# A Mamba block with a feed-forward layer: sines, rotation, carried states and the final sum rewritten on ScalarE and GpSimd

## The chip, the cores and the metric

The kernel runs on one core of a Trainium2 chip. The core's engines run side by side, each with its own queue of instructions in program order: TensorE (PE, with its weight loads as PEld), VectorE (DVE), ScalarE (ACT), GpSimd (POOL) and SyncE (SP), which here only issues DMAs. They wait for each other by semaphores. The metric is the device time of one execution in microseconds; the time before is the median of three runs.

## The reference

The input is x, 2 sequences of 4096 tokens of width 256. First a layer norm and a Mamba-like layer, then a feed-forward layer, each added to x through a further layer norm. What matters here:

```python
Bn = _rmsnorm(B_raw + B_bias, B_norm_w)
Cn = _rmsnorm(C_raw + C_bias, C_norm_w)
dt = softplus(dt_in * W_dt[:, 0] + b_dt)
freqs = softplus(rope_freqs)
angles = cumsum(mean(dt, axis=-1, keepdims=True), axis=1) * freqs
cos_a, sin_a = cos(angles), sin(angles)
# _rope, for B and for C, over pairs (ve, vo) of neighbouring states:
re = ve * cos_a - vo * sin_a
ro = ve * sin_a + vo * cos_a
# scan over the tokens, 512 channels x 16 states:
h = dA * h + u
y = sum(h * C, axis=-1)
...
x = x + layernorm(mamba(layernorm(x)))
x = x + layernorm(ffn(layernorm(x)))
```

So for each token there are 8 angles, and B and C have 16 states each, which are turned in 8 pairs. The last line is the final sum.

## The kernel before

**Blocks and units.** The tokens are cut into 16 blocks (NB) of T = 512, eight to a sequence. A block's scan is 64 units: 4 groups of 128 channels (j) x 4 rounds of states (q) x 4 (c). A unit is 128 partitions x 512 tokens: 32 channels x 4 states on the partitions, the tokens along the row.

**What a unit needs.** `decay` (L1021 on) lets ACT write the decay da = exp(dt * A) into PSUM; four such tiles exist, and it is made for the unit after the next one at most. `inputs` (L1030) lets POOL multiply b with v for two units into a tile g, of which there are three. `unit_scan` (L1043, L1046) runs the recurrence on DVE. For some units of a round (SPLIT) the scan stays in da and DVE multiplies by c (`product_v`, L1060, with the last column copied to hl by L1061); for the others POOL multiplies by c (`product_g`, L1056), and ACT copies the last column (`last`, L1050, tile hl). `sum_states` (L1072) adds up the states on PE, and thereby frees g. A sequence's later blocks start from the states that the block before left (hl): `carry` makes the tile ini, and `initial` (L1016) adds hl to it, one channel group at a time.

**Order.** It is written out by hand. Each unit has three places in a timetable; the tables AT, AT_FIRST and LAG say at which place of the running block each step of the *next* block (norm, projections, softplus, angles, sines, rotation, loads) and of the block *before* (output projection, feed-forward layer, final sum) is issued. Each engine takes its instructions in that order. SP issues all loads and stores of the loop in order too. `silu_z` stands at place 151, `sines` at 153, `rotate_a` at 155, `rotate_b` and `bc_turn` at 157, `bc_store` at 160; between 151 and 153 no decay is issued. `initial` is issued for channel group 0 at unit 0, and for group j + 1 at the first unit of the last round of group j.

**Sines and rotation.** DVE brings the angles into [-pi, pi] (`angles`, tile ang, 128 x 32: 4 x 128 tokens x 8 angles). ACT takes Sin of it (sn) and of half of it (cs); POOL makes the cosine, 1 - 2 sin^2 of the half angle, by L822 and L823, four products of 64 elements (L832 to L835), and the difference and sum into rot (L841, L842). L844 multiplies the turned B and C (bdotc). PE transposes rot (L850), ACT copies it (L854), and SP writes it to DRAM, from where the b and c of all units of the next block are loaded.

**Tables.** ACT evaluates functions from a table set that has to be loaded. `special` (L220 on) loads the set of Exp and Ln by hand (L223); for all other functions the load is put in automatically and stands under the line of the activation (L227).

**Final sum.** `finish` (L1208) lets POOL add o2 to the tile xpost, 512 elements a row at a time, and SP writes it out. xpost is loaded by `x_load`. The tiles of b and c begin two floats ahead of the data (L983 on, `t[:, 2:]`); xpost doesn't.

Of the kernel before, what the change touches and what calls it, by code (L numbers as in the profile page):

```python
# [8 lines left out]
F32 = mybir.dt.float32  # L9
AF = mybir.ActivationFunctionType  # L10
ALU = mybir.AluOpType
# [3 lines left out]
P = 128  # L15
G = 32
T = 512
NC4 = T // P
DM = 256
DI = 512  # L20
NJ = DI // P
NS = 16
NG = P // G
NQ = NS // NG
# [7 lines left out]
PI2_HI = 6.28125  # L32
PI2_MID = 0.0019350051879882812
PI2_LO = 3.0199159819567517e-07

GBUFS = 3
DA_PSUM = 4
# [136 lines left out]
def mamba_ffn_kernel(  # L174
# [25 lines left out]
    nc = tc.nc  # L200
    B, L, _ = x.shape
# [4 lines left out]
    small = ctx.enter_context(tc.tile_pool(name="small", bufs=2))  # L206
    p1 = ctx.enter_context(tc.tile_pool(name="p1", bufs=1))
# [10 lines left out]
    table = [None]  # L218

    def special(dst, src, f, **kw):  # L220
        if f in (AF.Exp, AF.Ln):
            if table[0] != "ln_exp":
                nc.scalar.preload_act_table_set("natural_log_exp_and_others")  # L223
            table[0] = "ln_exp"
        else:
            table[0] = f
        nc.scalar.activation(dst, src, f, **kw)  # L227

    def mm_tile(shape, name):
# [2 lines left out]
    def tokens(ap, k):  # L232
        b, t0 = k // NBLK, (k % NBLK) * T
        return ap[b, t0 : t0 + T, :].rearrange("(c p) d -> p c d", p=P)

    def x_load(k, tag):
        if tag == "h1":

            xt = p1.tile([P, NH, T], F32, tag="h1", name=f"xpre_{k}")
            xt = xt[:, 0:2, :].rearrange("p a (b d) -> p (a b) d", d=DM)  # L240
        else:
            xt = p1.tile([P, NC4, DM], F32, tag=tag, name=f"{tag}_{k}")
        nc.sync.dma_start(xt, tokens(x, k))
        return xt

# [14 lines left out]
    ones = const.tile([P, P], F32, name="ones")  # L260
# [364 lines left out]
    def new_block(k):  # L625
        s = Block()
        s.k, s.first = k, k % NBLK == 0
        s.bc_d = tc.dram_tile([2 * NS, T], F32, name=f"bc_d_{k}")
        s.dt_d = tc.dram_tile([DI, T], F32, name=f"dt_d_{k}")
        s.v_d = tc.dram_tile([DI, T], F32, name=f"v_d_{k}")  # L630
        s.pz, s.dt, s.dtT, s.dx, s.vs, s.ph, s.bcq, s.ch, s.g = {}, {}, {}, {}, {}, {}, {}, {}, {}
        s.p2, s.ff, s.pq, s.ps, s.ys = {}, {}, {}, {}, {}
        return s
# [157 lines left out]
    H = NS // 2  # L791

    def angles(s):
# [14 lines left out]
        nc.vector.tensor_scalar_sub(tn, turns, ROUND)  # L808
        for part in (PI2_HI, PI2_MID, PI2_LO):
            nc.vector.scalar_tensor_tensor(ang, tn, -part, ang, ALU.mult, ALU.add)  # L810
        nc.vector.tensor_scalar(s.ang, ang, -3.1415925, 3.1415925, ALU.max, ALU.min)

    def sines(s):
        k = s.k
        s.sn = small.tile([P, NC4, H], F32, tag="sn", name=f"sn_{k}")
        s.cs = small.tile([P, NC4, H], F32, tag="cs", name=f"cs_{k}")
        special(s.sn, s.ang, AF.Sin)
        special(s.cs, s.ang, AF.Sin, scale=0.5)

    def rotate_a(s):  # L820
        k, sn, cs = s.k, s.sn, s.cs
        nc.gpsimd.tensor_mul(cs, cs, cs)  # L822
        nc.gpsimd.tensor_scalar(cs, cs, -2.0, 1.0, ALU.mult, ALU.add)  # L823
        pairs = s.bc.rearrange("p c s (h two) -> p c s h two", two=2)
        ve, vo = pairs[:, :, :, :, 0], pairs[:, :, :, :, 1]
        snb = sn[:, :, None, :].to_broadcast([P, NC4, 2, H])
        csb = cs[:, :, None, :].to_broadcast([P, NC4, 2, H])
        s.tt = [
            small.tile([P, NC4, 2, H], F32, tag=f"t{i}", name=f"t{i}_{k}", bufs=1)
            for i in range(4)  # L830
        ]
        nc.gpsimd.tensor_mul(s.tt[0], ve, csb)  # L832
        nc.gpsimd.tensor_mul(s.tt[1], vo, snb)
        nc.gpsimd.tensor_mul(s.tt[2], ve, snb)
        nc.gpsimd.tensor_mul(s.tt[3], vo, csb)  # L835

    def rotate_b(s):
        k, tt = s.k, s.tt
        s.rot = small.tile([P, NC4, 2 * NS], F32, tag="rot", name=f"rot_{k}")
        rp = s.rot.rearrange("p c (s h two) -> p c s h two", s=2, two=2)  # L840
        nc.gpsimd.tensor_sub(rp[:, :, :, :, 0], tt[0], tt[1])  # L841
        nc.gpsimd.tensor_add(rp[:, :, :, :, 1], tt[2], tt[3])  # L842
        s.bdotc = small.tile([P, NC4, NS], F32, tag="bdotc", name=f"bdotc_{k}", bufs=1)
        nc.gpsimd.tensor_mul(s.bdotc, s.rot[:, :, 0:NS], s.rot[:, :, NS : 2 * NS])  # L844

# [145 lines left out]
    def load_ch(s, j, what):  # L991

        src = s.dt_d if what == "dtr" else s.v_d
        t = scan.tile([P, NG, T], F32, tag=what, name=f"{what}_{s.k}_{j}")
        for n in range(NG):
            nc.sync.dma_start(
                t[n * G : (n + 1) * G],
                src[j * P : (j + 1) * P, :].rearrange("(c i) t -> i c t", i=G),
            )
        s.ch[j, what] = t  # L1000
# [12 lines left out]

    def initial(s, prev, j):

        nc.gpsimd.tensor_add(s.ini[:, j], s.ini[:, j], prev.hl[:, j])  # L1016

    das = {}

# [366 lines left out]
    def plan_behind(s):  # L1386

        plan = Plan(AT, 3 * (s.k + 1) * NU)
        add = plan.add

        def begin():
            s.x = x_load(s.k, "xpost")
            s.sums = small.tile([P, NC4], F32, tag="hsum", name=f"hsum_{s.k}")

        def norm():

            s.nh = Norm(s.x, 1.0 + LN_EPS, LN_EPS * LN_EPS, f"h{s.k}")
            s.nh.stats((0, 1))

        add("x_load", begin)  # L1400
        for h in range(2):
            add("out_project", out_project, s, h, i=h)
            add("out_square", out_square, s, h, i=h)
            add("out_power", out_power, s, h, i=h)
            add("residual", residual, s, h, i=h)
        add("h_stats", norm, i=0)
        add("h_stats", lambda: s.nh.stats((2, 3)), i=1)
        add("h_power", lambda: s.nh.power())
        add("h_offset", lambda: s.nh.offset())
        for h in range(2):  # L1410
            add("h_apply", lambda h=h: s.nh.apply((2 * h, 2 * h + 1)), i=h)
        for h in range(2):
            add("h_turn", lambda h=h: s.nh.turn(h), i=h)
            add("h_evict", lambda h=h: s.nh.evict(h), i=h)
        for f in range(NH):
            add("ffn_1", ffn_1, s, f, i=f)
            add("ffn_keep", ffn_keep, s, f, i=f)
        for h in range(2):
            add("gelu", gelu, s, h, i=h)
        for c in range(NC4):  # L1420
            add("ffn_2", ffn_2, s, c, i=c)
            add("ffn_sums", ffn_sums, s, c, i=c)
            add("ffn_out", ffn_out, s, c, i=c)
            add("ffn_square", ffn_square, s, c, i=c)
            if c % 2 == 1:
                h = c // 2
                add("ffn_power", ffn_power, s, h, i=h)
                add("ffn_scale", ffn_scale, s, h, i=h)
                add("finish", finish, s, h, i=h)
        return plan.done()  # L1430
# [26 lines left out]
    for what, lags in LAG.items():  # L1457
        for u in range(len(units)):
            j, q, c = units[u][1:]
            n = SPLIT[q]  # L1460
# [48 lines left out]
    def at_place(place):  # L1509
        behind(place)  # L1510
        for plan in plans:
            plan.run(place)

    for base in range(NB * NU + BEHIND):
        k, m = base // NU, base % NU
        j, q, c = m // (NQ * NG), m // NG % NQ, m % NG
        cur, prev = blocks.get(k), blocks.get(k - 1)
        if m == 0:
            if k + 1 < NB:
                blocks[k + 1] = new_block(k + 1)  # L1520
                blocks[k + 1].xpre = xnext
                plans.append(plan_ahead(blocks[k + 1], cur))
            if 0 < k < NB:
                plans.append(plan_behind(prev))
        if cur is not None:
            if q == 0 and c == 0 and j == 0 and not cur.first:
                initial(cur, prev, 0)
            if m == (LOAD_FIRST if k + j == 0 else j * NQ * NG) and j < NJ - 1:
                load_ch(cur, j + 1, "dtr")
                load_ch(cur, j + 1, "vr")  # L1530
            if q == NQ - 1 and c == 0 and j < NJ - 1 and not cur.first:
                initial(cur, prev, j + 1)
        at_place(3 * base)
        if cur is not None:
            ahead(base + AHEAD_DA, "da", 1, decay)
            ahead(base + AHEAD_U, "u", 2, inputs)
        at_place(3 * base + 1)
        if cur is not None:
            unit_scan(cur, j, q, c)
        at_place(3 * base + 2)  # L1540
        if base == NB * NU - 10:
            tail_load(cur)
        if m == X_AT and k + 2 < NB:
            xnext = x_load(k + 2, "h1")
# [49 lines left out]
```

## Time and profile before

| | |
|---|---|
| median of three runs (2022.16 to 2025.43) | 2024.63 us |
| profiled execution | 2027.52 us |
| its span, first to last instruction | 2025.8 us |
| mean granted TensorE clock | 0.931 |
| one block in the steady part | about 117 us |
| busy in 117 us of it (873 to 990 us): PE, DVE, ACT, POOL | 103.89, 110.14, 100.10, 110.10 us |
| table loads: L223, L227, L564 | 80, 80, 1, of 1283 ns each |
| sn, cs: Sin of 128 x 32 elements | 213 ns each, 16 times |
| L822, L823 (128 x 32) | 239, 217 ns, 16 times |
| L832 to L835, L841, L842, L844 (128 x 64) | 319 to 325 ns, 16 times each |
| L1016 (128 x 16) | 223 ns, 56 times |

The page's fifth part has such groups: line, engine, operation, tile written and read with the elements of a row, count, busy time, mean of one, and the idle time of the engine just before, with what ended it. The fourth part follows the work that ended last back to what released it. A timeline row gives start and duration in us, and in brackets how long the engine stood still before it. Busy shares are averages over the whole span, with a prologue of some 55 us in which little runs on POOL and DVE, and a tail of some 60 us.

### The profile page before, as it was taken

Reading aid. Unit: us, or ns where it says so; the run is one execution under the profiler, and the core shown is the slowest. Engines: PE = TensorE matmul, PEld = TensorE weight load, DVE = VectorE, ACT = ScalarE, POOL = GpSimd, SP = SyncE. Lnnn points to the kernel's source line nnn. Section 1 sums busy time; section 2 is a strip of 40 time slices with the busy share of each in tenths; the row PEclk is TensorE's granted clock in tenths of the full one; section 3 lists DMA queues with packets and bytes.
Section 4 is the critical chain, followed back from the end, with each engine's and each line's share of the span. In section 5 each row is a group of like instructions: output and inputs, shape, how many; then the busy total and the mean of one; then the engine's idle time right before and its main releaser. Section 6 shows DMA issues by size and latency. Waiting matters only on the chain.

```text
span 2025.8 us, 28291 instructions
## 1 busy us (share of the span) xinstructions
PE 1739.3 (86%) x8670; PEld 1039.7 (51%) x8670; DVE 1769.0 (87%) x2834; ACT 1624.4 (80%) x3358; POOL 1786.3 (88%) x1171
## 2 busy tenths in 40 slices
PE   6776988898989989898898988898898989887688
PEld 3433555464645536464554646465464646545256
DVE  1778999999999989899998989999899999989861
ACT  4766887979888797888879788887979888796654
POOL 3688899999989999999999999999999989999970
PEclk7867999999999999999999999999999999999798
DMA  4734446364444635444464545346454534545300
GB/s 98 181 93 105 105 120 153 92 159 105 116 104 124 158 93 150 104 119 105 123 157 103 139 104 132 110 110 152 104 137 105 140 102 115 147 104 135 75 21 11
DMA packets 155722, 233.39 MB, mean 115 GB/s; under 512 B 30161, under 2 KB 55825, under 8 KB 155569
## 3 DMA queue, kind: packets, MB, share of 16 engines
q1 hardware_dynamic: 153440, 230.80, 45.6%
q0 software_dynamic: 544, 0.71, 0.3%
q8 instruction: 68, 1.11, 0.2%
q14 instruction: 86, 0.70, 0.1%
q10 hardware_dynamic: 1584, 0.07, 0.1%
HBM read 188.51 MB, written 42.99 MB: 114 GB/s over the span
## 4 chain that ended last, share of the span: by engine, by line
ACT 38%; DVE 18%; PE 13%; POOL 11%; DMA 10%; issue 7%; SPq 2%; DVEq 0%; ACTq 0%; POOLq 0%
ACT da L227 12%; DVE g L1046 6%; POOL g L1030 6%; DMA vr<-v_d 5%; ACT L227 5%; DVE da L1043 4%; ACT L223 3%; ACT h L1134 3%; DMA xpre<-in_L_attn_x_dram 2%; POOL g L1056 2%; ACT dt L227 2%; PE y L1072 2%; PE pdtT L779 2%; DVE g L1060 2%; PE pz L639 2%
## 5 line engine op out<-in xcount | busy, mean ns | idle before, releaser
L1030 POOL TENSOR_TENSOR g<-b,vr 128x1024 f32<-128x1024 f32 x512 | 1019.0, 2002 | 43.3 <-PE y L1072 15.6
L1046 DVE TENSOR_TENSOR_SCAN g<-da,ini,g 128x512 f32<-128x512 f32 x560 | 709.9, 1272 | 48.0 <-ACT da L227 37.2
L227 ACT ACTIVATE da<-dtr,aneg 128x512 f32<-128x512 f32 x1024 | 683.6, 683 | 83.7 <-DVE g L1046 46.2
L1056 POOL TENSOR_TENSOR g<-c,g 128x1024 f32<-128x1024 f32 (+1 forms) x256 | 627.3, 2453 | 63.4 <-ACT hl L1050 56.7
L1043 DVE TENSOR_TENSOR_SCAN da<-da,ini,g 128x512 f32<-128x512 f32 x336 | 421.9, 1274 | 39.4 <-POOL g L1030 23.1
L1072 PE MATMUL y<-g,fold 128*32 128x512 f32 x2048 | 339.5, 665 | 24.9 <-POOL g L1056 14.7
L1146 PE MATMUL pf<-w2q,h 128*128 128x257 f32 x1024 | 312.9, 387 | 18.2 <-DVE o L1184 14.9
L1123 PE MATMUL ph<-oT_h,w1q 128*128 128x512 f32 x480 | 242.1, 639 | 24.1 <-ACT oT_h L595 13.1
L639 PE MATMUL pz<-oT_a,wi 128*128 128x512 f32 x512 | 250.1, 626 | 10.2 <-ACT zs L657 4.9
L1060 DVE TENSOR_TENSOR g<-da,c 128x512 f32<-128x512 f32 x384 | 257.2, 670 | 0.0
L1155 PEld LDWEIGHTS pf<-h 128*128 128x128 f32 x1024 | 194.6, 190 | 27.2
L1155 PE MATMUL pf<-h 128*128 128x128 f32 x1024 | 196.7, 274 | 0.0
L1146 PEld LDWEIGHTS pf<-w2q,h 128*128 128x128 f32 x1024 | 155.1, 191 | 53.0 <-DVE o L1184 33.5
L639 PEld LDWEIGHTS pz<-oT_a,wi 128*128 128x128 f32 x512 | 92.9, 195 | 156.8 <-issue 88.1
L1123 PEld LDWEIGHTS ph<-oT_h,w1q 128*128 128x128 f32 x480 | 89.1, 201 | 156.2 <-issue 75.8
L1072 PEld LDWEIGHTS y<-g,fold 128*32 128x32 f32 x2048 | 49.1, 112 | 139.8 <-POOL g L1056 48.6
L1092 PE MATMUL po<-wo,zs 128*128 128x256 f32 x480 | 111.6, 386 | 0.0
L911 PE MATMUL ps<-mix,dtT 128*128 128x129 f32 (+1 forms) x512 | 79.3, 301 | 34.2 <-DVE remdot L879 27.0
L911 PE MATMUL pw<-ddot,dtT 128*128 128x128 f32 (+1 forms) x512 | 84.7, 315 | 27.5 <-DVE dx L974 23.2
L1092 PEld LDWEIGHTS po<-wo,zs 128*128 128x128 f32 x480 | 88.7, 190 | 36.8 <-issue 26.0
L1046 DVE TENSOR_TENSOR_SCAN g<-da,g 128x512 f32<-128x512 f32 x80 | 96.6, 1211 | 12.6 <-ACT da L227 12.2
L779 PE MATMUL pdtT<-ident,dt 128*128 128x128 f32 x256 | 54.6, 357 | 57.7 <-ACT dtT L787 32.6
(234 smaller groups left out, 2458.2 us busy)
## 6 DMA issues: line engine op xcount, KB each, us to landing
dtr<-dt_d SPq DMA_DIRECT2D x256, 256.0 KB, 5.0
vr<-v_d SPq DMA_DIRECT2D x256, 256.0 KB, 7.0
dt_d<-dt SPq DMA_DIRECT2D x64, 256.0 KB, 2.1
v_d<-v SPq DMA_DIRECT2D x64, 256.0 KB, 4.6
b<-bc_d SPq DMA_DIRECT2D x256, 64.0 KB, 2.1
c<-bc_d SPq DMA_DIRECT2D x256, 64.0 KB, 2.6
xpre<-in_L_attn_x_dram SPq DMA_DIRECT2D x16, 512.0 KB, 4.5
xpost<-in_L_attn_x_dram SPq DMA_DIRECT2D x15, 512.0 KB, 3.9
```

The costliest lines, as they stand in the source:

```text
L227: nc.scalar.activation(dst, src, f, **kw)
L639: nc.tensor.matmul(s.pz[e], lhsT=wi[:, kk, e * P : (e + 1) * P], rhs=s.na.oT[:, kk, :], start=(kk == 0), stop=(kk == 1),)
L1030: nc.gpsimd.tensor_mul(s.g[j, q][:, hs, :], s.bcq[0, q][:, None, :].to_broadcast([P, 2, T]), s.ch[j, "vr"][:, hs, :],)
L1043: nc.vector.tensor_tensor_scan(da, da, g, ini, ALU.mult, ALU.add)
L1046: nc.vector.tensor_tensor_scan(g, da, g, ini, ALU.mult, ALU.add)
L1056: nc.gpsimd.tensor_mul(g, s.bcq[1, q][:, None, :].to_broadcast([P, NG - n, T]), g)
L1060: nc.vector.tensor_mul(s.g[j, q][:, c, :], da, s.bcq[1, q])
L1072: nc.tensor.matmul(s.ys[j][c * G : (c + 1) * G, :], lhsT=fold, rhs=g[:, c, :], start=False, stop=(q == NQ - 1), skip_group_check=True,)
L1092: nc.tensor.matmul(s.p2[h][:, i, :], lhsT=s.zs[j][:, c * P : (c + 1) * P], rhs=wo[:, j, :], start=(j == 0), stop=(j == NJ - 1),)
L1123: nc.tensor.matmul(s.ph[f], lhsT=w1q[:, kk, f * P : (f + 1) * P], rhs=s.nh.oT[:, kk, :], start=(kk == 0), stop=(kk == 1),)
L1146: nc.tensor.matmul(po[:, 0 : DM + 1], lhsT=gT, rhs=w2q[:, f, :], start=(f == 0), stop=(f == NH - 1), skip_group_check=True,)
L1155: nc.tensor.matmul(po[:, DM + 1 :], lhsT=gT, rhs=gT, start=False, stop=False, skip_group_check=True,)
```

## The change

1. `special` loads by hand also "silu_and_others" for Silu and Sin.
2. `sines` makes on ACT what the rotation needs: sn holds -sin and sin side by side, cs the cosine twice, both 16 wide. That is three Sin, a Square and an Identity with scale -2 and a bias of 1. `rotate_a` and `rotate_b` are then four POOL operations: the whole of B and C times the cosine (128 elements), the swapped halves times -sin and sin (two of 64), and one sum (128).
3. `initial` adds group 0 as before and groups 1 to 3 in one operation, at the last round of group 0.
4. xpost begins two floats into its tile, so that it and o2 are 8 bytes apart in the row.

No entry of the timetable is changed.

```diff
+TABLES = {
+    AF.Exp: "natural_log_exp_and_others",
+    AF.Ln: "natural_log_exp_and_others",
+    AF.Silu: "silu_and_others",
+    AF.Sin: "silu_and_others",
+}
...
     def special(dst, src, f, **kw):
-        if f in (AF.Exp, AF.Ln):
-            if table[0] != "ln_exp":
-                nc.scalar.preload_act_table_set("natural_log_exp_and_others")
-            table[0] = "ln_exp"
-        else:
-            table[0] = f
+        name = TABLES.get(f)
+        if name is not None and table[0] != name:
+            nc.scalar.preload_act_table_set(name)
+        table[0] = name or f
         nc.scalar.activation(dst, src, f, **kw)
...
-            xt = p1.tile([P, NC4, DM], F32, tag=tag, name=f"{tag}_{k}")
+            xt = p1.tile([P, NC4 * DM + 2], F32, tag=tag, name=f"{tag}_{k}")
+            xt = xt[:, 2:].rearrange("p (c d) -> p c d", d=DM)
...
     def sines(s):
         k = s.k
-        s.sn = small.tile([P, NC4, H], F32, tag="sn", name=f"sn_{k}")
-        s.cs = small.tile([P, NC4, H], F32, tag="cs", name=f"cs_{k}")
-        special(s.sn, s.ang, AF.Sin)
-        special(s.cs, s.ang, AF.Sin, scale=0.5)
+        s.sn = small.tile([P, NC4, H, 2], F32, tag="sn", name=f"sn_{k}", bufs=1)
+        s.cs = small.tile([P, NC4, H, 2], F32, tag="cs", name=f"cs_{k}", bufs=1)
+        special(s.sn[:, :, :, 0], s.ang, AF.Sin, scale=-1.0)
+        special(s.sn[:, :, :, 1], s.ang, AF.Sin)
+        half = small.tile([P, NC4, H], F32, tag="half", name=f"half_{k}", bufs=1)
+        special(half, s.ang, AF.Sin, scale=0.5)
+        nc.scalar.activation(half, half, AF.Square)
+        nc.scalar.activation(
+            s.cs, half[:, :, :, None].to_broadcast([P, NC4, H, 2]), AF.Identity, scale=-2.0, bias=ones[:, 0:1]
+        )
...
     def rotate_a(s):
-        nc.gpsimd.tensor_mul(cs, cs, cs)
-        nc.gpsimd.tensor_scalar(cs, cs, -2.0, 1.0, ALU.mult, ALU.add)
...
-        nc.gpsimd.tensor_mul(s.tt[0], ve, csb)
-        nc.gpsimd.tensor_mul(s.tt[1], vo, snb)
-        nc.gpsimd.tensor_mul(s.tt[2], ve, snb)
-        nc.gpsimd.tensor_mul(s.tt[3], vo, csb)
+        nc.gpsimd.tensor_mul(s.tt[0], s.bc, cs[:, :, None, :].to_broadcast([P, NC4, 2, NS]))
+        for i in range(2):
+            nc.gpsimd.tensor_mul(
+                turned_pairs[:, :, :, :, i],
+                pairs[:, :, :, :, 1 - i],
+                sn[:, :, None, :, i].to_broadcast([P, NC4, 2, H]),
+            )
...
     def rotate_b(s):
-        nc.gpsimd.tensor_sub(rp[:, :, :, :, 0], tt[0], tt[1])
-        nc.gpsimd.tensor_add(rp[:, :, :, :, 1], tt[2], tt[3])
+        nc.gpsimd.tensor_add(
+            s.rot.rearrange("p c (s n) -> p c s n", s=2), tt[0], tt[1]
+        )
...
     def initial(s, prev, j):
-        nc.gpsimd.tensor_add(s.ini[:, j], s.ini[:, j], prev.hl[:, j])
+        js = slice(j, j + 1) if j == 0 else slice(j, NJ)
+        nc.gpsimd.tensor_add(s.ini[:, js], s.ini[:, js], prev.hl[:, js])
...
-            if q == NQ - 1 and c == 0 and j < NJ - 1 and not cur.first:
+            if q == NQ - 1 and c == 0 and j == 0 and not cur.first:
                 initial(cur, prev, j + 1)
```

More of the change, by code (lines that the diff above doesn't have):

```diff
@@ L814, in sines @@
         k = s.k
-        s.sn = small.tile([P, NC4, H], F32, tag="sn", name=f"sn_{k}")
-        s.cs = small.tile([P, NC4, H], F32, tag="cs", name=f"cs_{k}")
-        special(s.sn, s.ang, AF.Sin)
-        special(s.cs, s.ang, AF.Sin, scale=0.5)
+        s.sn = small.tile([P, NC4, H, 2], F32, tag="sn", name=f"sn_{k}", bufs=1)
[8 more added lines that the diff above has]
+        )
     def rotate_a(s):
-        k, sn, cs = s.k, s.sn, s.cs
-        nc.gpsimd.tensor_mul(cs, cs, cs)
-        nc.gpsimd.tensor_scalar(cs, cs, -2.0, 1.0, ALU.mult, ALU.add)
+        k, sn = s.k, s.sn
+        cs = s.cs.rearrange("p c h two -> p c (h two)")
         pairs = s.bc.rearrange("p c s (h two) -> p c s h two", two=2)
-        ve, vo = pairs[:, :, :, :, 0], pairs[:, :, :, :, 1]
-        snb = sn[:, :, None, :].to_broadcast([P, NC4, 2, H])
-        csb = cs[:, :, None, :].to_broadcast([P, NC4, 2, H])
         s.tt = [
-            small.tile([P, NC4, 2, H], F32, tag=f"t{i}", name=f"t{i}_{k}", bufs=1)
-            for i in range(4)
-        ]
-        nc.gpsimd.tensor_mul(s.tt[0], ve, csb)
-        nc.gpsimd.tensor_mul(s.tt[1], vo, snb)
-        nc.gpsimd.tensor_mul(s.tt[2], ve, snb)
-        nc.gpsimd.tensor_mul(s.tt[3], vo, csb)
+            small.tile([P, NC4, 2, NS], F32, tag=f"t{i}", name=f"t{i}_{k}", bufs=1) for i in range(2)
+        ]
+        turned_pairs = s.tt[1].rearrange("p c s (h two) -> p c s h two", two=2)
+        nc.gpsimd.tensor_mul(s.tt[0], s.bc, cs[:, :, None, :].to_broadcast([P, NC4, 2, NS]))
[5 more added lines that the diff above has]
+            )
     def rotate_b(s):
@@ L839, in rotate_b @@
         s.rot = small.tile([P, NC4, 2 * NS], F32, tag="rot", name=f"rot_{k}")
-        rp = s.rot.rearrange("p c (s h two) -> p c s h two", s=2, two=2)
-        nc.gpsimd.tensor_sub(rp[:, :, :, :, 0], tt[0], tt[1])
-        nc.gpsimd.tensor_add(rp[:, :, :, :, 1], tt[2], tt[3])
+        nc.gpsimd.tensor_add(
+            s.rot.rearrange("p c (s n) -> p c s n", s=2), tt[0], tt[1]
+        )
         s.bdotc = small.tile([P, NC4, NS], F32, tag="bdotc", name=f"bdotc_{k}", bufs=1)
```

## The prediction

> **What bounds the kernel now.** I read the busy shares, then the chain of waits, then one block (about 117 us) instruction by instruction.
>
> ```profile
> PE 1739.3 (86%) x8670; PEld 1039.7 (51%) x8670; DVE 1769.0 (87%) x2834; ACT 1624.4 (80%) x3358; POOL 1786.3 (88%) x1171
> ...
> ACT 38%; DVE 18%; PE 13%; POOL 11%; DMA 10%; issue 7%; SPq 2%; DVEq 0%; ACTq 0%; POOLq 0%
> ```
>
> By busy time POOL leads, and the change takes POOL work away. But POOL holds only 11% of the chain that ended last; ACT holds 38%, and the change gives work to ACT. So the question is which engine the others wait for where the work moves. The timeline around the sines of one block (start, duration; in brackets the idle time before and what ended it):
>
> ```profile
> 289.55 1.29 ACT L227 ACTIVATE da<-dtr,aneg 128x512 f32<-128x512 f32 x2
> 290.86 1.28 ACT L227 ACT_TABLE_LOAD   x1
> 292.15 2.19 ACT L227 ACTIVATE zs<-zs 128x512 f32<-128x512 f32 x4
> 294.25 0.21 ACT L227 ACTIVATE sn<-ang 128x32 f32<-128x32 f32 x1
> 294.37 0.21 ACT L227 ACTIVATE cs<-ang 128x32 f32<-128x32 f32 x1
> 294.60 1.28 ACT L223 ACT_TABLE_LOAD   x1
> 295.90 0.69 ACT L227 ACTIVATE da<-dtr,aneg 128x512 f32<-128x512 f32 x1
> ...
> 292.58 2.00 POOL L1030 TENSOR_TENSOR g<-b,vr 128x1024 f32<-128x1024 f32 x1
> 294.66 0.24 POOL L822 TENSOR_TENSOR cs<-cs 128x32 f32<-128x32 f32 x1
> ...
> 297.37 2.00 POOL L1030 TENSOR_TENSOR g<-b,vr 128x1024 f32<-128x1024 f32 x1
> ...
> 296.69 1.29 DVE L1043 TENSOR_TENSOR_SCAN da<-da,ini,g 128x512 f32<-128x512 f32 x1 [0.39 <-ACT hl L1050]
> ...
> 323.30 1.58 PE L911 MATMUL pw<-ddot,dtT 128*128 128x127 f32 x8 [2.02 <-DVE dx L974]
> 327.27 0.75 DVE L974 SCALAR_TENSOR_TENSOR dx<-pw,dsk,xp 128x512 f32<-128x512 f32 x1 [0.87 <-PE pw L962]
> 328.43 3.95 POOL L1030 TENSOR_TENSOR g<-b,vr 128x1024 f32<-128x1024 f32 x2 [0.98 <-POOL g L1030]
> 338.20 0.69 ACT L227 ACTIVATE da<-dtr,aneg 128x512 f32<-128x512 f32 x1 [1.71 <-DVE hl L1061]
> ```
>
> From 290.86 to 295.90 ACT makes no decay (da). DVE uses up those it has, then stands 0.39 us before the scan at 296.69. The row names ACT's hl, but hl ends at 296.70; the da before it ends at 296.59, so the wait is for da. In every later block that I opened at this place the same wait stands there. What follows it on DVE:
>
> ```profile
> 296.69:326.40 29.71, 25.00 (x169) 20.64 (x169) 29.57 (x52) 22.01 (x60) 29.63 (x20) 0.96 0.60 150
> ```
>
> In these columns (length, PE, PEld, DVE, ACT, POOL, clock, DMA) DVE is busy 29.57 of 29.71 us: a delay at 296.69 isn't made good. At its end PE's pw waits for dx and dx for pw, so this gap moves along; PE's next sum frees the g buffer for which POOL stands 0.98 us. At 338.20 ACT waits for DVE, at 346.23 DVE 0.84 us for ACT's da, at 354.35 ACT 0.68 us for DVE; then ACT has no gap until 381.42 (1.89 us for PE's pdtT, which waited for ACT's dtT), and goes on to the next sines at 412.62. **The ring is ACT, DVE, ACT, and no POOL instruction lies on it.** POOL waits in this block 0.98, 1.61, 0.82, 0.45, 1.36, 0.44, 0.90 and 0.85 us, always for the ring. Against this speaks that the printed chain runs through POOL from 294.66 to 312 and then through a DMA; both paths end within 0.5 us of each other near 328, and the rival below is built on that.
>
> **The change part by part.**
>
> *Silu's table for Sin.* The page ScalarE: Activation LUTs of the Trainium skill (What ACT_TABLE_LOAD costs) prices each change of set at about 2.66 us, load and drain; its rule is to group functions by set. If Sin had a load of its own in 15 blocks, 15 x 2.66 = 40 us of ACT would go, or 15 x 1.28 = 19 us by this trace's load. The rows above have none between zs and sn: the one load at 290.86 serves both. Only in block 0 does Sin load alone (40.16 us, in time in which ACT then waits 1.35 us for ang), and there a load is still needed. I count 0.
>
> *Sines on ACT.* Before, sn and cs end 0.12 + 0.21 = 0.33 us after sn starts. After: two Sin writing every second element and a third for the half angle, each starting 0.12 after the one before: the third ends at 0.12 + 0.12 + 0.21 = 0.45. The Square needs it: the pair rsf after rsf shows a gap of 0.02 to 0.03, and 32 elements take 0.21 as Sin does, so 0.69. The Identity needs the Square and has a bias operand: L373 (one such operand, 256 elements) takes 494 ns; 192 elements fewer at 0.84 ns (from 512 elements in 614 and 2048 in 1911) leaves 333: end at 1.05. **Added: 0.72 us**, and the table load and da behind them start that much later. Bounds: without a price for the bias operand (aneg, 64 elements, 256 ns) 0.64; with 0.06 us more on each of three strided or dependent steps 0.90. That the strided write costs more is in no row; I take the plain one. Nothing covers it: what queues behind is the load and the da for which DVE already stands idle.
>
> *Rotation on POOL.* L822 to the next L1030 is now 297.37 - 294.66 = 2.71 us. After: a product of 128 elements (403 to 456 ns by L743 and L744, say 0.43), two of 64 (0.32), a sum of 128 that waits for them (0.08 gap, as L822 to L823, and 0.43), and bdotc (0.08 and 0.32), independent ones overlapping by 0.045: 1.86 us, so 0.85 saved (0.7 to 0.95). But the first product needs cs, the last thing ACT makes, 0.72 later, and POOL is already there: L1030 ends at 294.58 with cs. So POOL gains 0.85 - 0.72 = **0.13 us a block**; rot itself comes 0.1 earlier for bc_turn and bc_store.
>
> *States in front.* L1016, 16 elements, 223 ns, four a block in 14 blocks, 0.175 apart. After: one such and one of 48 elements, 223 + 32 x 1.6 = 274 ns (slope from 16 elements in 223 to 128 in 404): saved 4 x 0.175 - 0.175 - 0.23 = 0.3 us a block. What the merged one reads was written a dozen units earlier, so no wait is added. One removed at 370.96 stands just ahead of the only place where DVE waits for POOL (371.04, 0.93 us); DVE then waits 1.90 us for ACT's da at 382.80, which takes this gain away.
>
> *Final sum.* The groups give a price for operands 8 bytes apart:
>
> ```profile
> L1056 POOL TENSOR_TENSOR g<-c,g 128x1536 f32<-128x1536 f32 x128 | 372.1, 2907 | 38.7 <-ACT hl L1050 33.1 <-DMA xpost<-in_L_attn_x_dram 3.6
> L1056 POOL TENSOR_TENSOR g<-c,g 128x1024 f32<-128x1024 f32 x128 | 255.9, 1999 | 24.7 <-ACT hl L1050 23.6 <-DMA dtr<-dt_d 0.7
> L1208 POOL TENSOR_TENSOR xpost<-o,xpost 128x512 f32<-128x512 f32 x30 | 38.3, 1277 | 0.0
> L420 POOL TENSOR_TENSOR wide<-wide 128x1024 f32<-128x1024 f32 x4 | 9.4, 2350 | 5.9 <-issue 3.8 <-DVE wide L415 2.1
> ```
>
> c is read 8 bytes into its tile, g at its start: 1024 elements in 1999 ns, and (2907 - 1999)/512 = 1.77 ns an element. L420, no operand shifted, takes 2350. So L1208 should fall from 1277 to 1999 - 512 x 1.77 = 1.09 us: 0.18 saved, 0.37 a block in 15 blocks (between 0, if the shift helps only as b and c have it, and 0.37). It lies at 318 to 323, and POOL stands 0.98 us at 328: hidden. The DMAs into and out of the shifted tile are off the ring; b and c land in shifted tiles too, in 2.1 to 2.6 us.
>
> **Sum.** POOL loses 16 x 0.85 + 14 x 0.3 + 15 x 0.37 = 23 us of busy time and nearly none of it ends anything. ACT gains 16 x 0.72 = 11.5 us. On the ring stand blocks 2 to 15: 14 x 0.72 = +10.1. Block 0's rotation is in series in the prologue: -0.1. Block 1's sines fall where ACT has slack (it waits 1.94 us at 179.50) and POOL comes 1.2 us after cs: up to -0.85, of which I take half; I leave the last block's share at 0. No DMA is moved; SP's load of b at 312.04, which waits for POOL's last product, is issued 0.13 earlier, and what it carries isn't on the ring. That is **+9.5 us** on a span of 2025.8, which with 1.7 us around it is the profiled 2027.52. The median of the runs is 2024.63, so 2034.1, 0.47% slower.
>
> **The rivals.**
> 1. *Slower as summed*, chance 0.64. With 0.64 to 0.90 us a block, +8.5 to +12 us: 2032 to 2038, with some slip 2030 to 2039.
> 2. *POOL's path ends last near 328, so it is faster*, 0.16. If DVE's delay is absorbed before POOL's next L1030, each of 15 blocks gains 0.13 + 0.37 + 0.3 = 0.8 us: -12, 2012.6. For it: POOL is the busiest engine, and the printed chain goes through the rotation to 312 us, where SP's load of b waits for the last product. Against it: DVE has 0.14 us idle in 29.7. It decides from 0.72 us of slack on DVE between 297 and 328.
> 3. *No change*, 0.13. The delay of da is half absorbed, say 0.3 of 0.72 left, while POOL's rotation and final sum give 0.3 back: 2022 to 2028.
> 4. *More than summed*, 0.07. ACT's strided writes cost double or a later issue order slips (x loads, v_d writes): over +16 us, 2041 and up.
>
> That Sin would load a table after all, against the silu set, is the change not doing what it says: 15 x 1.28 us more, within case 4.
>
> **Numbers.** Likeliest 2034.1. A range of 2016 to 2040 holds case 1, case 3, a third of case 2, and leaves out the rest of 2 and case 4; case 1 alone is 2030 to 2039. A difference of 0.2% (4 us) is about what the measurement tells from none. Faster 0.16, same 0.14, slower 0.70.
>
> **What would show it.** Right: 161 table loads as before; from sn's start to the load behind the sines 1.05 to 1.1 us instead of 0.35; the DVE wait at the scan behind it about 1.1 us instead of 0.39; POOL busy down by some 20 us while its waits for hl and y grow; the period of a block up by 0.7. Wrong: DVE's wait at that scan unchanged, or DVE idle between there and dx, or a shorter period with POOL's wait before the L1030 behind dx gone.

## The result, and the profile after

The changed kernel took 2039.18 us (median of 4 runs, 2037.65 to 2041.84), before beside it 2024.29 us (4 runs): ratio 1.0065, interval 1.0048 to 1.0082, so **14.9 us slower**. A second comparison on another occasion (e11 below) gave +10.3 us. Of the 4.6 us between the two, 3.3 are in before (2024.29 from 4 runs here, 2027.58 from 9 there) and 1.3 in the changed kernel. The profiled execution spans 2038.3 us, 12.5 more than before's, at a clock of 0.93 (0.931 before).

The page of the changed kernel, busy time and the chain of waits:

```profile
PE 1746.8 (86%) x8670; PEld 1043.8 (51%) x8670; DVE 1767.8 (87%) x2834; ACT 1635.0 (80%) x3406; POOL 1768.5 (87%) x1079
...
ACT 40%; DVE 21%; PE 18%; DMA 10%; issue 7%; POOL 3%; SPq 1%; DVEq 0%; ACTq 0%; POOLq 0%
```

POOL lost 17.8 us of busy time and nearly left the chain (11% to 3%); ACT gained 10.6 us; DVE did as much as before. The shares of ACT, DVE and PE in the chain grew. The busiest engine got shorter and the kernel longer.

The timeline of the changed kernel around the sines of the same block as in the prediction (line numbers are now 5 to 14 higher: decay's L227 is L232, the load L223 is L230, POOL's L1030 is L1044, the scan L1043 is L1057):

```profile
294.98 0.34 ACT L232 ACTIVATE sn<-ang 128x32 f32<-128x32 f32 x2
295.21 0.21 ACT L232 ACTIVATE half<-ang 128x32 f32<-128x32 f32 x1
295.46 0.23 ACT L829 ACTIVATE half<-half 128x32 f32<-128x32 f32 x1
295.72 0.35 ACT L830 ACTIVATE cs<-half,ones 128x64 f32<-128x64 f32 x1
296.09 1.28 ACT L230 ACT_TABLE_LOAD   x1
297.38 0.69 ACT L232 ACTIVATE da<-dtr,aneg 128x512 f32<-128x512 f32 x1
...
298.18 1.29 DVE L1057 TENSOR_TENSOR_SCAN da<-da,ini,g 128x512 f32<-128x512 f32 x1 [1.16 <-ACT hl L1064]
...
296.14 0.46 POOL L842 TENSOR_TENSOR t<-bc,cs 128x128 f32<-128x128 f32 x1 [0.84 <-ACT cs L830]
...
298.12 2.00 POOL L1044 TENSOR_TENSOR g<-b,vr 128x1024 f32<-128x1024 f32 x1
```

From the first sine to the load ACT now takes 1.11 us (0.35 before). The decay behind the load is as much later, and DVE's wait before the scan that needs it is 1.16 us instead of 0.39. POOL stands 0.84 us for the cosine; it takes 1.98 us from there to its next large product instead of 2.71, and that product starts 3.14 us after the first sine, where it started 3.12 after it.

What the groups of the changed kernel say of the new operations (mean of one in ns behind the busy time):

```profile
L1222 POOL TENSOR_TENSOR xpost<-o,xpost 128x512 f32<-128x512 f32 x30 | 32.7, 1090 | 0.0
L844 POOL TENSOR_TENSOR t<-bc,sn 128x64 f32<-128x64 f32 x32 | 10.6, 352 | 0.0
L842 POOL TENSOR_TENSOR t<-bc,cs 128x128 f32<-128x128 f32 x16 | 7.4, 460 | 14.4 <-ACT cs L830 14.4
L830 ACT ACTIVATE cs<-half,ones 128x64 f32<-128x64 f32 x16 | 5.6, 348 | 0.5
```

The final sum fell from 1277 to 1090 ns. All of the 14.4 us that POOL stands before L842 is for cs, 0.9 us a block.

**Where the time came from.** I took the start of each of the 1024 scans on DVE, after less before. Here are three blocks of it, in us, at some of their 64 units (worked out from the two traces):

```
unit            44     48     52     56     60
block 1       0.72   0.72   1.48   1.42   2.85
block 7       6.85   6.86   7.62   7.49   7.36
block 12     11.08  11.09  11.85  11.78  13.20
```

Two things are seen. Between units 48 and 52, the place behind the sines, each of the blocks 1 to 14 (they carry the sines of blocks 2 to 15) loses 0.76 us; some 0.07, at most 0.31, comes back by unit 56. From 48 to 56 the 14 blocks lose **9.5 us** together. And in 6 of the 14 blocks another **1.43 us** is lost between 56 and 60. Block 1 is one of them. The windows of both kernels there (busy time of PE, PEld, DVE, ACT and POOL, then granted clock), before first:

```profile
298.00:301.00 3.00, 2.60 (x15) 2.38 (x16) 3.00 (x7) 2.97 (x6) 3.00 (x2) 1.00 0.11 27
301.00:304.50 3.50, 3.50 (x27) 3.29 (x25) 3.50 (x4) 1.35 (x4) 3.50 (x3) 1.00 0.29 85
```

and the changed kernel:

```profile
298.00:301.00 3.00, 1.55 (x10) 1.11 (x9) 2.83 (x5) 2.90 (x10) 3.00 (x3) 0.97 0.01 3
301.00:304.50 3.50, 3.50 (x13) 3.02 (x12) 3.50 (x7) 1.65 (x3) 3.50 (x3) 0.54 0.17 47
```

TensorE was granted half its clock from 300.8 to 304.2 us and got 13 matmuls done instead of 27. The timeline of PE in the changed kernel shows what came ahead of it:

```profile
299.89 0.70 PE L1160 MATMUL pf<-w2q,h 128*128 128x257 f32 x2 [1.45 <-DVE o L1198]
...
301.78 1.07 PE L1160 MATMUL pf<-w2q,h 128*128 128x257 f32 x2
```

and in before:

```profile
298.40 0.70 PE L1146 MATMUL pf<-w2q,h 128*128 128x257 f32 x2 [0.68 <-DVE o L1184]
299.16 0.60 PE L1146 MATMUL pf<-w2q,h 128*128 128x257 f32 x2
```

PE waits for the feed-forward layer's last step on DVE, which queues behind the delayed scan: its pause is 1.45 us instead of 0.68. At half clock the same pair of matmuls takes 1.07 us instead of 0.60, and the burst ends late.

### The profile page after: what moved, and what is told of

Same layout as the page of the kernel before. It is cut to its first block, busy times and chain, and to the rows that moved or that the text cites. A ratio compares the mean times of both kernels' runs of the same rounds, so it can differ in the third digit from the quotient of the medians.

```text
span 2038.3 us, 28248 instructions
## 1 busy us (share of the span) xinstructions
PE 1746.8 (86%) x8670; PEld 1043.8 (51%) x8670; DVE 1767.8 (87%) x2834; ACT 1635.0 (80%) x3406; POOL 1768.5 (87%) x1079
## 3 DMA queue, kind: packets, MB, share of 16 engines
q8 instruction: 68, 1.11, 0.2%
## 4 chain that ended last, share of the span: by engine, by line
ACT 40%; DVE 21%; PE 18%; DMA 10%; issue 7%; POOL 3%; SPq 1%; DVEq 0%; ACTq 0%; POOLq 0%
ACT da L232 13%; DVE g L1060 7%; DVE da L1057 6%; ACT L230 5%; DMA vr<-v_d 5%; PE pf L1160 4%; ACT L232 3%; ACT h L1148 3%; PE y L1086 3%; ACT dt L232 2%; DVE g L1074 2%; PE pf L1169 2%; DMA xpre<-in_L_attn_x_dram 2%; PE pdtT L786 2%; POOL g L1044 2%
## 5 line engine op out<-in xcount | busy, mean ns | idle before, releaser
L1044 POOL TENSOR_TENSOR g<-b,vr 128x1024 f32<-128x1024 f32 x512 | 1018.1, 2002 | 54.9 <-PE y L1086 21.6
L232 ACT ACTIVATE da<-dtr,aneg 128x512 f32<-128x512 f32 x1024 | 683.7, 683 | 83.6 <-DVE g L1060 43.2
L1060 DVE TENSOR_TENSOR_SCAN g<-da,ini,g 128x512 f32<-128x512 f32 x560 | 710.0, 1272 | 46.8 <-ACT da L232 36.6
L1057 DVE TENSOR_TENSOR_SCAN da<-da,ini,g 128x512 f32<-128x512 f32 x336 | 421.5, 1273 | 46.1 <-POOL g L1044 22.4
L1160 PE MATMUL pf<-w2q,h 128*128 128x257 f32 x1024 | 320.3, 395 | 26.7 <-DVE o L1198 23.2
L1169 PEld LDWEIGHTS pf<-h 128*128 128x128 f32 x1024 | 199.4, 195 | 29.4
L1169 PE MATMUL pf<-h 128*128 128x128 f32 x1024 | 200.8, 279 | 0.0
```

The source lines that it names most:

```text
L1044: nc.gpsimd.tensor_mul(s.g[j, q][:, hs, :], s.bcq[0, q][:, None, :].to_broadcast([P, 2, T]), s.ch[j, "vr"][:, hs, :],)
L1057: nc.vector.tensor_tensor_scan(da, da, g, ini, ALU.mult, ALU.add)
L1060: nc.vector.tensor_tensor_scan(g, da, g, ini, ALU.mult, ALU.add)
L1160: nc.tensor.matmul(po[:, 0 : DM + 1], lhsT=gT, rhs=w2q[:, f, :], start=(f == 0), stop=(f == NH - 1), skip_group_check=True,)
L1169: nc.tensor.matmul(po[:, DM + 1 :], lhsT=gT, rhs=gT, start=False, stop=False, skip_group_check=True,)
```

## The experiments

All were timed against before in the same sessions. The medians of before were 2027.48 to 2027.9 us for e1 to e12, and 2024.29 us for after. "Step" is the median over blocks 1 to 14 of what the scans lose (gain, if negative) between the units named, against the profile of before; "1.4 us" is in how many of the 14 blocks the loss of some 1.4 us between 56 and 60 stands.

| kernel | median us | ratio, interval | step 48-52 | step 52-56 | 1.4 us |
|---|---|---|---|---|---|
| after | 2039.18 | 1.0065, 1.0048 to 1.0082 | +0.76 | -0.07 | 6 |
| e1 rotation only | 2046.23 | 1.0087, 1.0073 to 1.0100 | +0.76 | -0.07 | 7 |
| e2 the others only | 2024.16 | 0.9984, 0.9976 to 0.9992 | 0 | 0 | 1 |
| e3 sines first | 2040.75 | 1.0068, 1.0054 to 1.0081 | +0.76 | -0.07 | 8 |
| e4 ACT longer | 2045.50 | 1.0088, 1.0075 to 1.0101 | +0.89 | -0.07 | 7 |
| e5 POOL longer | 2041.28 | 1.0070, 1.0058 to 1.0082 | 0 | +0.82 | 0 |
| e6 silu in one | 2022.56 | 0.9981, 0.9974 to 0.9988 | -0.28 | +0.16 | 0 |
| e7 e6 and e2 | 2019.73 | 0.9962, 0.9949 to 0.9975 | -0.28 | +0.17 | 0 |
| e8 square and cosine on POOL | 2025.80 | 0.9992, 0.9984 to 1.0000 | +0.12 | -0.07 | 1 |
| e9 both longer | 2047.98 | 1.0096, 1.0080 to 1.0111 | +0.89 | -0.06 | 3 |
| e10 both shorter | 2014.99 | 0.9939, 0.9926 to 0.9951 | -0.28 | -0.18 | 0 |
| e11 after again | 2037.86 | 1.0049, 1.0035 to 1.0062 | +0.76 | -0.07 | 3 |
| e12 after, silu in one | 2036.32 | 1.0038, 1.0025 to 1.0050 | +0.48 | -0.07 | 6 |

**e1 and e2: the change in two halves.** e1 is before with the new `sines`, `rotate_a` and `rotate_b` alone; e2 is after with these three as before.

> Before, with the sines and the rotation of the change alone. Theory A (0.75 us more on ACT behind the sines delays the decay for which DVE already stands): 14 blocks x 0.75 = +10.5 us, 2033 to 2037, the scan behind the sines 0.75 us later in every block from the third on, POOL about 0.96 us idle ahead of the rotation. Theory B (the loss comes from the other parts: the merged states, the shifted tile and its DMAs): within 3 us of before.

> The change without its sines and rotation: table by hand, merged states, shifted xpost. Theory A: POOL loses some 9 us of busy time, all of it in waits, so 2021 to 2027, no change beyond 3 us. Theory B: +10 us and more. The rival that POOL's path ends last: 15 x 0.67 = 10 us faster, 2014.

The loss is the rotation's: e1 has the same step and is 18.7 us slower, e2 has no step at all and is 3.4 us faster. The step of e1 is what theory A expected; its time, 2046.23, is 9 us above the 2033 to 2037 expected, with the 1.4 us loss in 7 blocks. e2 took 10.3 us off POOL's busy time for these 3.4; where they come from I could not place, since its gains stand in the first block and in single jumps elsewhere.

**e3: the sines ahead of silu of z**, so that the cosine is there long before POOL asks for it; ACT's work up to the load stays the same.

```diff
-    "sines": (153,),
+    "sines": (151,),
...
-        add("silu_z", silu_z, s, range(NJ))
         add("sines", sines, s)
+        add("silu_z", silu_z, s, range(NJ))
```

> The change with the five ACT instructions of the sines in front of the four of silu_z, so that cs is there 2.2 us earlier; ACT's work between its two table loads is the same. Theory A: as the change, 2036 to 2042, although POOL no longer stands ahead of the rotation (14 us less idle there). If POOL's wait for cs were the cost: back to 2024 or below, to 2014 with POOL's savings.

The timeline of e3, at the same place:

```profile
292.81 0.46 POOL L842 TENSOR_TENSOR t<-bc,cs 128x128 f32<-128x128 f32 x1
...
295.72 1.29 DVE L1057 TENSOR_TENSOR_SCAN da<-da,ini,g 128x512 f32<-128x512 f32 x1 [1.16 <-ACT da L232]
```

POOL has no wait for cs any more; DVE's wait is still 1.16 us and the step still 0.76. So POOL's wait for the cosine, the most visible new wait of the page (14.4 us), is not the cost. The row also names its releaser as da here: the wait that was put down to hl was for the decay.

**e4: ACT longer, without the change.** Two copies of 336 elements on ACT behind the two sines of before, POOL as it was.

```diff
         special(s.cs, s.ang, AF.Sin, scale=0.5)
+        pad = p1.tile([P, 512], F32, tag="pad", name=f"pad_{k}")
+        for _ in range(2):
+            nc.scalar.activation(pad[:, 0:336], wi[:, 0, 0:336], AF.Copy)
```

> Before, with two copies of 336 elements on ACT behind the sines, which nothing reads: ACT 0.76 us longer there, POOL, DVE, PE and SP as before. Theory A: 14 x 0.76 = +10.6 us, 2033 to 2037, the same step between unit 48 and 52 of each block as in the change. The rival that POOL's rotation is the path: no change, since cs is not later.

The timeline of e4 at the same place:

```profile
293.48 0.98 ACT L821 ACTIVATE pad<-wi 128x336 f32<-128x336 f32 x2
...
296.57 1.29 DVE L1046 TENSOR_TENSOR_SCAN da<-da,ini,g 128x512 f32<-128x512 f32 x1 [1.28 <-ACT hl L1053]
```

The wait is 1.28 us where before has 0.39, and the step is 0.89 us. ACT's length behind the sines alone makes the step, with the rotation of before. The time is +17.9 us, where 14 x 0.76 = +10.6 were expected: the steps make 11.3 of it, and the 1.4 us loss stands in 7 blocks.

**e5: POOL longer, without the change.** Two products of 128 elements ahead of bdotc. They took some 0.95 us, where 0.72 were expected.

```diff
+        pad = p1.tile([P, 512], F32, tag="pad", name=f"pad_{k}")
+        for _ in range(2):
+            nc.gpsimd.tensor_mul(pad[:, 0:128], wi[:, 0, 0:128], wi[:, 0, 128:256])
         s.bdotc = small.tile([P, NC4, NS], F32, tag="bdotc", name=f"bdotc_{k}", bufs=1)
```

> Before, with two products of 128 elements on POOL behind the rotation's sum, which nothing reads: POOL 0.72 us longer at the very place where ACT's pad cost 18 us, ACT as before. Theory A (the ring is ACT and DVE, POOL has 0.8 to 1.0 us of waits near the end of that stretch): 0 to +3 us. The rival that POOL's path ends last there: 15 x 0.72 = +11 us.

This is where theory A fell: +13.8 us, not 0 to 3. The step stands elsewhere, between units 52 and 56. The timeline of e5 there:

```profile
305.04 2.00 POOL L1033 TENSOR_TENSOR g<-b,vr 128x1024 f32<-128x1024 f32 x1
...
307.07 1.29 DVE L1046 TENSOR_TENSOR_SCAN da<-da,ini,g 128x512 f32<-128x512 f32 x1 [0.80 <-POOL g L1033]
```

and the same two rows in before:

```profile
301.28 3.95 POOL L1030 TENSOR_TENSOR g<-b,vr 128x1024 f32<-128x1024 f32 x2
...
303.31 1.29 DVE L1043 TENSOR_TENSOR_SCAN da<-da,ini,g 128x512 f32<-128x512 f32 x1
```

In before the first of the two products ends at 301.28 + 2.00 = 303.28 and the scan of unit 56 starts at 303.31, as soon as DVE is done with its own queue. **Two paths arrive there together**: ACT's decay by way of DVE, and POOL's rotation by way of its products. No wait stands in the row, so no idle time betrays it.

**e6, e7: ACT shorter.** Silu of z in one activation of 2048 elements (1.91 us in the trace) instead of four of 512 (2.19 us), on before and on e2. The four tiles of z become one (zall).

```diff
...
-        for j in js:
-            special(s.zs[j], s.zs[j], AF.Silu)
+        special(s.zall, s.zall, AF.Silu)
```

> Before, with silu_z as one activation of 2048 elements instead of four of 512, so that ACT is 0.28 us shorter between its two table loads (2.19 to 1.91 us): the dose with the other sign. Theory A: -14 x 0.28 = -4 us. Rival (only an added wait costs, ACT's time there is otherwise hidden): no change.

> The same one activation, on top of the change without its sines and rotation. Theory A and the small gain of the other parts add: -4 - 3.4 = -7 us, 2020 if before is at 2027.6, faster than both kernels.

ACT's 0.28 us come through at unit 52, and 0.16 of it is lost again by unit 56, which is what the tie of e5 says: POOL is now last. Both are faster than before, e6 by 4.9 us and e7 by 7.75 us. The steps left at unit 56 make only 1.9 us of e6's gain (1.7 of e7's); where the rest arises was not traced.

**e8: the square and the cosine back on POOL**, the three sines left on ACT.

> The change with the Square and the 1 - 2 s^2 back on POOL (the second one writes the 16 wide cosine): ACT keeps three Sin, 0.13 us more than before instead of 0.75; POOL has six operations and busy time about as before. Theory A: 14 x 0.13 = +2 us, less the 3.4 of the other parts: -2 to +1 us. Rival (what costs is the wait of POOL or the strided writes of sn, not ACT's length): +8 us and more, as the change.

ACT then adds only the third sine (step 0.12) and the time is that of before within 0.2%. Against e2, which has the same other parts, it is 1.6 us slower; 14 x 0.12 is 1.7. The square and the cosine on ACT are the cost of the change.

**e9: both longer**, the additions of e4 and e5 in one kernel.

> Before with the two copies on ACT behind the sines and the two products on POOL behind the rotation's sum together; apart they gave +17.9 us (0.885 us a block at units 48 to 52) and +13.8 us (0.82 us a block at units 52 to 56). Theory A, ACT and POOL are two paths that run beside each other and end within about 0.1 us of each other at the scan of unit 56, so that the later one counts: about 0.9 to 1.0 us a block, +14 to +20 us over before. Theory B, the delays add, since both lie on one path in series: 1.7 us a block, +27 to +33 us.

The steps are those of e4 alone, +0.89 and -0.06: POOL's 0.82 vanishes in ACT's. The time, +20.1 us, is just above what theory A expected and far from B's. The later of the two paths counts, not their sum.

**e10: both shorter**, e7 with the bdotc product behind POOL's next large products, and with it the sum on DVE that reads it (`dot_sum`).

```diff
-    "dot_sum": (167,),
+    "dot_mul": (168,),
+    "dot_sum": (174,),
...
+    def dot_mul(s):
+        s.bdotc = small.tile([P, NC4, NS], F32, tag="bdotc", name=f"bdotc_{s.k}", bufs=1)
+        nc.gpsimd.tensor_mul(s.bdotc, s.rot[:, :, 0:NS], s.rot[:, :, NS : 2 * NS])
...
```

> The kernel of e7 (silu of z in one activation, and the change without its sines and rotation) with the product for the dot sum moved behind POOL's next large product and the dot sum on DVE moved behind it, so that POOL's row ahead of the scan of unit 56 is about 0.3 to 0.4 us shorter. e7 won 0.28 us a block at unit 52 and gave 0.17 back at unit 56. Theory A, what it gave back was POOL's product coming last: now at most 0.05 is given back, the scan of unit 56 starts some 0.2 to 0.28 us earlier in each block than in before, and the kernel comes to 9 to 12 us below before. Theory B, DVE itself or ACT's next decay took it: the same 0.17 is given back and the time is that of e7, 7 to 8 us below before.

The scan of unit 56 in e7, where DVE stands for POOL:

```profile
299.69 3.96 POOL L1039 TENSOR_TENSOR g<-b,vr 128x1024 f32<-128x1024 f32 x2
...
301.73 1.29 DVE L1052 TENSOR_TENSOR_SCAN da<-da,ini,g 128x512 f32<-128x512 f32 x1 [0.15 <-POOL g L1039]
```

and in e10, where the product is ready (302.89 + 2.00 = 304.89) and nothing is waited for:

```profile
302.89 2.00 POOL L1043 TENSOR_TENSOR g<-b,vr 128x1024 f32<-128x1024 f32 x1
...
304.99 1.27 DVE L1056 TENSOR_TENSOR_SCAN da<-da,ini,g 128x512 f32<-128x512 f32 x1
```

Nothing is given back at 56, as POOL's product no longer comes last. Another 0.18 is gained there and 0.20 is lost by unit 60. That is DVE's sum over bdotc, which stood ahead of unit 56 in before (first row) and stands ahead of unit 60 in e10 (second row):

```profile
303.14 0.19 DVE L862 TENSOR_REDUCE dot<-bdotc 128x4 f32<-128x64 f32 x1
...
308.60 0.21 DVE L874 TENSOR_REDUCE dot<-bdotc 128x4 f32<-128x64 f32 x1
```

So the edit moved work on both engines. Moving the sum on DVE alone could not have been enough: in e7 POOL's product ends at 299.69 + 2.00 = 301.69, and the scan waits for it until 301.73. **2014.99 us, 12.9 less than before and the fastest of all.** That is a little more than theory A expected, and the steps (14 x 0.26 = 3.6 us at unit 60) explain only a part of it; the remainder stands in jumps of 1.0 to 1.4 us in other stretches, and I have not traced it.

**e11 and e12: the size, and the same edit where POOL isn't last.** e11 is the changed kernel again; e12 is the changed kernel with e6's edit.

> The changed kernel itself, beside more runs of before on one chip. Measured was +14.9 us from four runs of each; the steps behind the sines in the trace make 14 x 0.755 = 10.6 us. Theory A, the steps are the whole of it and the rest came from the few runs of before: +9.5 to +12.5 us here. Theory B, the changed timetable falls worse on the stretches of halved TensorE clock as a rule: +14 to +17 us here too.

> The changed kernel with silu of z in one activation of 2048 elements, which takes 0.28 us a block from ACT ahead of the sines. On before the same edit was worth 0.12 us a block, since POOL came last once ACT was earlier. Theory A, in the changed kernel ACT is 0.7 us later than before and POOL is not last there: the whole 0.28 comes through, the step at units 48 to 52 is +0.47 instead of +0.755, nothing is given back at unit 56, and the kernel is 14 x 0.28 = 3.9 us (3 to 5) faster than the changed kernel of the same call. Theory B, POOL, which waits for cs, is last there as well: 1.7 us or less faster, with some 0.16 given back at unit 56.

e11: +10.3 us, as theory A has it. That the steps are the whole of it is not shown by this: e11's own profile has 9.5 us of steps and three losses of 1.43 us, and its last scan is only 11.3 us late, so other places gave some back. The two comparisons of the changed kernel overlap (1.0048 to 1.0082, 1.0035 to 1.0062), so its price is some 10 to 15 us. e12's step is 0.48 instead of 0.76 and nothing is given back at 56; the wait before the scan is 0.88 us, 0.28 less:

```profile
295.79 1.29 DVE L1058 TENSOR_TENSOR_SCAN da<-da,ini,g 128x512 f32<-128x512 f32 x1 [0.88 <-ACT hl L1065]
```

So in its place the mechanism is A's. The time isn't: 1.5 us less than e11, where A expected 3 to 5; the intervals of the two overlap, and e12's profile has the 1.4 us loss in 6 blocks against 3 in that of e11.

**The 1.4 us losses.** They fall in 42 blocks of all these profiles, and in each of the 42 a stretch of half TensorE clock covers 3.3 to 3.4 us between units 53 and 56; in none of the other 154 blocks is there such a stretch in that place. The seven kernels whose step at 52 is 0.48 us or more have them in 40 of 98 blocks, the other six and before in 2 of 98. So a longer pause of PE there goes with a halved clock behind it.

Which of the long pauses are followed by it depends on where they fall. In each of the 14 executions every edge of the clock record, but for the end of the record itself, lies within 0.03 us of one grid of 3.413 us, and the grid lies differently from execution to execution. PE's pause ahead of the burst of pf is 0.98 us or longer in 102 of the 196 blocks. In 41 of these a line of the grid falls between 0.2 us before and 1.02 us behind the end of the pause, and all 41 have the loss; of the other 61 one has it (block 14 of e9, a pause of 1.93 us). Of the 94 blocks with a pause of 0.83 us or less none has it. So it is in part chance how many blocks of one kernel lose 1.4 us: 6 in the profile of after, 3 in that of e11.

This is a pattern over 14 profiles, not an experiment: no run changed PE's pause alone. It isn't the whole account either. In the profile of after, 9.5 us of steps, 6 x 1.43 = 8.6 us of these losses and 0.7 us by the start of block 1 (0.0 in e11) make 18.8 us, but the last scan is 14.1 us late; the difference is regained where before had its own half-clock stretches or where other jumps fall.

## Why the prediction was right, and where it was not

- **Side and place: right.** The table loads are 113 + 47 + 1 = 161, as before. A change of set takes 1.29 us in the rows above, from the load at 296.09 to the decay at 297.38, and not the 2.66 us with a drain that the prediction also reckoned with; as no load was saved, nothing hangs on it. The cost is the decay behind the load: e1, e4 and e8 show that ACT's length there decides, e3 that POOL's wait doesn't.
- **Added on ACT, 0.72 us a block: 0.76 measured.** The terms of the sum held: Square 229 ns, Identity 348 where 333 was estimated, and the sine written to every second element takes 213 ns, as the plain one did, so on ACT the strided write cost nothing. 14 x 0.72 = 10.1 became 14 x 0.76 = 10.6, of which 1.2 come back by unit 56: 9.5 net in the trace.
- **"The ring is ACT, DVE, ACT, and no POOL instruction lies on it": wrong.** By e5 POOL's rotation is on a second path which ends within 0.1 us of the ring at unit 56; e6, e9 and e10 show the same from other sides. The prediction had seen the printed chain run through POOL and set it against DVE's idle time of 0.14 us in 29.7; but a path that arrives in time leaves no idle row. Nor was the 0.93 us at 371.04 the only wait of DVE for POOL in that block: another of 0.16 us stands at 374.31. It did no harm to the forecast, but that is luck: this change makes ACT later and POOL, against the first sine, neither later nor earlier. An edit that lengthens POOL's rotation would have been forecast as free, as e5 was.
- **POOL's gain of 0.13 us a block: not there.** The products of 64 elements, which now read and write every second element, take 352 ns instead of 322, and the rotation 1.98 us instead of 1.86, so 0.73 was saved and 0.76 lost to the later cosine. POOL's busy time fell by 17.8 us where 23 were summed; e1 and e2 put the miss at the rotation (10.1 us where 16 x 0.85 = 13.6 were expected) and not at the other parts (10.3 for 9.7). This split is rough: the halves make 20.4 and not 17.8, and e6 and e4, with POOL's work as before, have 1785.0 and 1787.7 us.
- **Final sum, 1.09 us: 1090 ns.** Hidden, as forecast, in the sense that no step appears for it; e2 as a whole is worth 3.4 us where the sum had about nothing.
- **Block 1's half share of 0.85:** no such step is seen there.
- **The sum, +9.5 us, is the size of the steps; a term for TensorE's clock is missing.** That the two agree to the tenth is luck: the sum took off 0.5 us for blocks 0 and 1, which isn't seen, and didn't know of the 1.2 us that come back. The prediction followed DVE's delay to ACT and POOL and left out that PE's burst of pf waits for DVE as well. That pause is 0.77 us longer, and it goes with half-clock stretches behind which 1.43 us are lost each time. Steps and losses together make 18.1 us in the profile of after and 13.8 us in that of e11; the measured +14.9 and +10.3 lie between this and the steps alone. What the term is worth in the end isn't shown.
- **The size.** 2039.18 is 5 us above the likeliest 2034.1, above the 2032 to 2038 of the first case, and close to the upper end of the whole range, 2040. +14.9 us is more than that case's +8.5 to +12 and less than the fourth's +16; e11's +10.3 lies inside the first.
- **The rivals.** "POOL's path ends last near 328, so it is faster" had a true core, POOL's path does matter, but it needs ACT's to stay: in after ACT is the later of the two by 0.7 us. "No change" needed half of the delay absorbed; 0.07 of 0.76 is, in most blocks.

## What to carry to other kernels

Work moved off the busiest engine was worth nothing here, where two engines' paths arrive together, and what the receiving engine gained in length counted almost in full, as the last wait there was for it. So look up, at the place where the work moves, what each input of the next instruction was waiting for and by how much the others were ahead, rows without a wait included. To gain at such a tie, shorten both paths (e10), and measure the tie by lengthening each path alone before deciding which one to work on. A delay that makes TensorE pause can cost more than itself: here a pause 0.77 us longer went, in some blocks, with a stretch of half clock and 1.43 us lost behind it, and how many blocks were hit changed between executions of the same kernel.

## What the hardware showed beyond expectation

- In the clock record each stretch at half clock, but for the last, which the record's end cuts short, lasts a whole number of 3.413 us (3.4, 6.8, 10.2, up to 37.5 in the prologue); before has 46 of them, after 51. The Trainium skill, TensorE: Matmul & The Clock Gate (What's actually happening) names a free-running window of 3413 ns, which agrees with the grid of these traces. By its table there an idle window of about 3.4 us lowers the clock; here PE stood still no longer than 1.45 us at a time and was busy 1.55 of 3.00 us ahead of the stretch at 300.8, and the clock was halved behind it.
- Beginning xpost 8 bytes into its tile took POOL's sum of 512 elements from 1277 to 1090 ns. In e1 and e4, without this edit, it takes 1272 and 1275 ns; in e2, with it, 1089.
- Four Silu of 512 elements cost 0.28 us more than one of 2048, and with POOL's row shortened too that led to the fastest kernel.
